# Reordering within a step of a graph attention and mixture-of-experts kernel: place transposes, factor products and counts later on TensorE, factor sums and tile results earlier on VectorE

## The chip, the core and the metric

The kernel runs on one core of a Trainium2 chip. A core has five engines with a queue of instructions each: TensorE (PE in the profile, its weight loads PEld), VectorE (DVE), ScalarE (ACT), GpSimd (POOL) and SyncE (SP), which here only starts transfers. The metric is the device time of one execution in microseconds (us), the median of several runs.

## The reference

6250 nodes with 256 features and 100000 edges go through a graph attention layer with two heads of 128 features, and then through a feed-forward layer in which every node is given to one of eight experts. Cut to what matters:

```python
x = x + gnn(layernorm(x))           # 6250 x 256
x = x + ffn(layernorm(x))

# gnn: Wh = x @ W_w + W_b, two heads of 128
e     = leaky_relu(s[src] + t[dst])     # s, t: one number per node and head
alpha = softmax of e over the edges of one src
agg   = segment_sum(alpha * Wh[dst], src)
out   = where(deg > 0, agg, Wh)

# ffn
H      = gelu(x @ W1 + b1)              # 6250 x 1024
probs  = softmax(H @ Wg + bg)           # 8 experts
assign = argmax(probs)
out    = probs[assign] * (H @ Wd[assign] + bd[assign])
```

## The kernel before

All main work is in `common_path`. A second function, `general_path`, is entered only for inputs that the first can't do, and isn't run here.

First, a start stage of some 115 us sorts the edges by source and writes a table of the projected nodes (260 numbers a row) to DRAM. Then the nodes are taken in 49 blocks of 128 source nodes. For every block the kernel needs up to 15 ranks of edges: rank t holds one edge for each of 128 lanes. GpSimd gathers the destination rows of each rank from the table with an indirect transfer (`fetch`, L788, L792), in three portions of five ranks. Of the 15 ranks 12 are taken straight from a sorted window; the last three, the "late ranks", collect what didn't fit and are picked out by products on TensorE.

The pieces of a block that the change concerns are these:

- `gather_late` (L733): six matmul instructions (three products) that move late edges to their lanes (tile pm, L738).
- `choose` (L740, L745 to L756): VectorE picks the late edges out; ScalarE casts their places into `loc` (L756).
- `spread` (L758): TensorE transposes the places of all 15 ranks (L761), ScalarE casts them to lT (L763), SyncE writes them to DRAM (lrow, L765) and reads them back for all partitions (lbc, L767).
- `compare` (L769, L771): VectorE turns lbc into a mask of ones and zeros, in place. There is a single buffer for lbc.
- `factors` (L773, L779): 15 small products of the mask with the source nodes' terms. `factor_sums` (L782, L786): VectorE adds the three pieces of each product.
- `count_pairs` (L685, L691): eight products that count edges to frequent destinations, from masks that `pick_pairs` (L677, L681 and L682) made.
- `compare_back` and `weigh` (L806, L814) on VectorE and ScalarE weight the gathered rows with the factor sums; `add_up` (L828, L833) sums them on TensorE into the block's result; `finish` (L836) normalizes it.

Four blocks make a phase k of the feed-forward layer: norm (`g_norm`), turns (`g_turn`, L903, that is, transposes of the normalized tokens), the hidden layer (`g_hidden`, L916), the experts' logits (`g_logits`, L954, `g_fold`, L966), the choice of expert (`g_choose`, `g_count`, `g_place`), and then turned rows (`g_rows`, L1039 and L1040) that `g_send` scatters into a list for each expert in DRAM. Tiles of 128 rows of those lists are read back (`w_load`, L1126), turned (`w_turn`, L1039), multiplied with the expert's weights (`w_expert`, L1144 and L1146), and finished on VectorE by `w_out` (L1158 and L1160, result y), whose result `w_wait` stores. PSUM tiles named pf, three in number, serve all of this part: each turn, product or count takes one and gives it back when another engine has read it. PSUM tiles named pm, two in number, serve the late ranks, places, factors and counts.

The order of the work is written out by hand. `at(slot, place, fn, ...)` files every piece under a step (slot) and a place within the step; the list is sorted by both, and each engine runs its instructions in that order. Block b stands at u = 3b, so that a block takes three steps and a phase twelve; v is the step in which phase k begins. The pieces of many blocks share a step: for instance, in every third step `spread` of one block stands beside `add_up` of an earlier one and, in one step of twelve (v+1), beside the token turns of a phase (place 38) and the turned rows of the phase before (places 38 and 39). On ScalarE, the copies of the turned rows and the rest of a row (L1040, L1055) have the places of their rows, the turned tokens (L908) have 45, and the cast in `choose` has 16. In steps v+7 and v+10 `g_fold` and `g_count` (36) and more turned rows (38) meet `spread`. Tiles of a phase are turned in steps 5, 7, 9 and 11 of the next phase's twelve, and their `w_out` follows two steps later.

Of the kernel before, what the change touches and what calls it, by code (L numbers as in the profile page):

```python
# [36 lines left out]
def common_path(  # L37
# [57 lines left out]
    NPH = -(-(NB - 1) // FB) + 1  # L95
# [98 lines left out]
    with ExitStack() as edges:  # L194
# [3 lines left out]
        def at(slot, place, fn, *args):  # L198
            plan.append((slot, place, len(plan), fn, args))
# [311 lines left out]
        for i, (d, flip) in enumerate(steps):  # L511
            t = 11 + 1.7 * i if i < 18 else 41.6 + 1.02 * (i - 18)
# [16 lines left out]
        for f0, f1, t0, step in ((n0, n1, 8.0, 0.7), (n4, NB - 1, 15, 2.0)):  # L529
            for j, b in enumerate(range(f0, f1)):  # L530
                c = b % CH
                t = t0 + step * (j - 0.5 * c)
# [11 lines left out]
        for b in range(NB):  # L544
            t = XN0 + NODE * b
# [374 lines left out]
        def blocks_of(k):  # L920
            return range(max(0, (k - 1) * FB + 1), min(NB, k * FB + 1))
# [268 lines left out]
        for b in range(NB):  # L1190
            u = 3 * b
            at(u - 6, 46, window, b)
            at(u - 4, 24, measure, b)
            at(u - 4, 43, prefix, b)
            at(u - 3, 5, prefix_out, b)
            at(u - 3, 12, split, b)
            at(u - 3, 33.7, gather_late, b)
            at(u - 2, 17, pick_pairs, b)
            at(max(u - 1, -0.2), 63, load_terms, b)
            at(u, 56, scale_terms, b, 0)  # L1200
            at(u + 1, 56, scale_terms, b, 1)
            at(u, 34, count_pairs, b)
            at(u + 2, 51, weigh_pairs, b)
            at(u + 4, 31, add_pairs, b)
            at(u - 2, 16, choose, b)
            at(u - 2, 33.5, spread, b)
            at(u, 9, compare, b)
            at(u, 33, factors, b)
            at(u + 1, 47, factor_sums, b)
            at(u + 4, 62, owned, b)  # L1210
            at(u + 6, 13, owned_biased, b)
            for q in range(3):
                at(u + q, 30, fetch, b, q)
                at(u + q + 1, 48, compare_back, b, q)
                at(u + q + 1, 50, weigh, b, q)
                at(u + q + 3, 32, add_up, b, q)
            at(u + 6, 14, finish, b)

        worked = n_off = 0
        u = [3 * blocks_of(k)[-1] + 6 for k in range(NPH)]  # L1220
        for k in range(NPH):
            bs = blocks_of(k)
            v = u[k]
            last = k == NPH - 1
            at(v, 34 if last else 51, g_norm, k)
            for i in range(-(-len(bs) // 2)):
                at(v + 0.5 * i, 52, g_xn, k, i)
                at(v + 1, 38 + 0.1 * i, g_turn, k, i)
                at(v + 1, 45 + 0.1 * i, g_turned, k, i)
            for q in range(4):  # L1230
                at(v + 2 + q, 20, g_hidden, k, q)
            at(v + 6, 19, g_logits, k)
            at(v + 6, 56, g_logits_out, k)
            at(v + 7, 36, g_fold, k)
            at(v + 8, 12, g_bias, k)
            at(v + 8, 35 if last else 51, g_max, k)
            at(v + 8, 58, g_exp, k)
            at(v + 9, 35 if last else 51, g_choose, k)
            at(v + 10, 36, g_count, k)
            at(v + 11, 35 if last else 51, g_place, k)  # L1240
            for i in range(len(bs)):
                t, p = (((v + 6, 40), (v + 6, 41), (v + 8, 60), (v + 8, 61))[i] if last else
                        ((v + 10, 38), (v + 11, 38), (v + 13, 38), (v + 13, 39))[i])
                at(t, p, g_rows, k, i)
                at(max(t, v + 10), p, g_rest, k, i)
                at(v + 14 if i > 1 and not last else v + 12, 44, g_send, k, i)
            rows_in = min(N, (bs[-1] + 1) * P)
            n = (TILES if last else max(0, (rows_in - LAG) // P)) - worked
            worked += n
            if n == 0:  # L1250
                continue
            assert n <= NMAX
            n_off += n if k < NPH - 2 else 0
            todo = tabulate(k, n, last)
            for i in range(2):
                at(*((v + 12, 35) if last else (v + 12 + 3 * i, 53)), next, todo)
            for i in range(n):
                t = v + 15 + i if last else u[k + 1] + (5 + 8 * i // n if k < NPH - 2 else (10, 11, 12, 13, 14)[i])
                at(t - 1 if last else t - 2 if k == NPH - 2 else max(t - 3, v + 15), 46 if last else 64, w_load, k, i)
                at(t, 21, w_turn, k, i)  # L1260
                at(t + 1, 22, w_expert, k, i)
                at(t + 2, 30 if k < NPH - 2 else 36, w_out, k, i)
                at(t + 2, 45, w_send if k >= NPH - 2 else w_wait, k, i)
        at(v + 18, 47, judge)
        for j in range(-(-n_off // 2)):
            t = 3 * NB + 4 + j + (7 if j > 9 else 0)
# [7 lines left out]
@with_exitstack  # L1274
def gat_then_ffn_kernel(
    ctx: ExitStack,
    tc: tile.TileContext,
    x: bass.AP,
    src: bass.AP,
    dst: bass.AP,  # L1280
    W: bass.AP,
    Wb: bass.AP,
    a: bass.AP,
    W1: bass.AP,
    b1: bass.AP,
    Wg: bass.AP,
    bg: bass.AP,
    Wd: bass.AP,
    bd: bass.AP,
    out: bass.AP,  # L1290
):
    keep = ctx.enter_context(tc.tile_pool(name="keep", bufs=1))
    odd = keep.tile([1, 1], I32, name="odd")
    common_path(tc, x, src, dst, W, Wb, a, W1, b1, Wg, bg, Wd, bd, out, odd)
    flag = tc.nc.values_load(odd[0:1, 0:1], min_val=0, max_val=1,  # L1295
                             skip_runtime_bounds_check_because="a flag, 0 or 1")
    with tc.If(flag > 0):
        general_path(tc, x, src, dst, W, Wb, a, W1, b1, Wg, bg, Wd, bd, out)
# [506 lines left out]
```

## Time and profile before

| | us |
|---|---|
| median of 3 runs | 1344.82 |
| lowest and highest | 1343.49, 1346.52 |
| the profiled execution | 1348.73 |
| its span (first to last instruction) | 1346.9 |
| mean granted TensorE clock | 0.924 |

| stage of the span, us | PE busy | DVE busy | ACT busy | POOL busy |
|---|---|---|---|---|
| 60 to 120 | 43.40 | 46.72 | 42.10 | 6.71 |
| 300 to 400 | 81.21 | 76.20 | 52.20 | 76.40 |
| 700 to 800 | 90.88 | 75.30 | 57.31 | 75.67 |
| 1100 to 1200 | 91.88 | 74.33 | 56.52 | 68.58 |
| 1250 to 1300 | 47.05 | 11.91 | 11.89 | 23.95 |

A line of waits reads "engine, tile, line <- what ended the wait: us in total, times, longest". A line of the timeline reads "start, duration, engine, line, operation, output<-input, number of instructions", and in brackets the idle time before it and what ended that. L761 means line 761 of the kernel. "issue" is time in which the engine waited for nothing that the profile shows. The start stage ends at about 115 us, the gathers end at 1194.1 us, and the rest is the last phase's feed-forward work.

### The profile page before, as it was taken

The numbers are of one execution on the slowest core, as the hardware profiler recorded it, in microseconds if no ns is written. First come the engines' busy times: TensorE is split into PE (matmuls) and PEld (weight loads), VectorE is DVE, ScalarE is ACT, GpSimd is POOL, SyncE is SP. The second block draws the span as 40 slices with busy tenths as digits, with TensorE's granted clock in tenths as the row PEclk, the third lists the DMA queues.
The fourth block names the chain that finished last, engine by engine and source line by source line (L and its number), as shares of the span: only waits on it lengthen the run. The fifth ranks groups of instructions, "written<-read, shape, count | busy, mean of one in ns | idle before, by whom it ended". The sixth has DMA issues, their size and how long they took to land. (4 is left out here: it accounts for less than half of the span.)

```text
span 1346.9 us, 22461 instructions
## 1 busy us (share of the span) xinstructions
PE 1130.7 (84%) x6404; PEld 864.5 (64%) x6404; DVE 945.8 (70%) x3521; ACT 694.2 (52%) x2060; POOL 877.9 (65%) x990
## 2 busy tenths in 40 slices
PE   4683667777986998989979989899898998998997
PEld 3462555556674775775856757757676677585785
DVE  6986877868687787786777876968777779652311
ACT  4683344544645455546465565564645555645321
POOL 0005777777777777776777777777776767736362
PEclk9796887897997998998999999999998899899998
DMA  4764776765656566665766656666657566646871
GB/s 143 220 198 133 228 208 168 207 195 152 187 156 204 182 204 181 221 180 178 219 208 186 216 172 199 198 203 202 213 178 208 158 193 190 182 155 236 296 251 54
DMA packets 118428, 257.91 MB, mean 191 GB/s; under 512 B 24254, under 2 KB 70538, under 8 KB 118152
## 3 DMA queue, kind: packets, MB, share of 16 engines
q0 software_dynamic: 46544, 137.57, 34.2%
q1 hardware_dynamic: 64440, 111.76, 26.3%
q10 hardware_dynamic: 7312, 7.05, 1.6%
q8 instruction: 55, 0.90, 0.3%
q14 instruction: 77, 0.63, 0.2%
HBM read 205.03 MB, written 57.98 MB: 195 GB/s over the span
## 5 line engine op out<-in xcount | busy, mean ns | idle before, releaser
L792 POOL DMA_INDIRECT wg<-table,dsti x735 | 717.0, 976 | 238.4 <-issue 190.4
L833 PE MATMUL p_a<-wg,hot 128*128 128x258 f32 x1470 | 365.5, 399 | 0.0
L833 PEld LDWEIGHTS p_a<-wg,hot 128*128 128x128 f32 x1470 | 286.5, 201 | 52.0 <-issue 9.2
L826 ACT ACTIVATE wg<-wg 128x128 f32<-128x128 f32 x735 | 230.9, 390 | 4.8
L916 PE MATMUL pf<-xT,w_sb 128*128 128x512 f32 (+1 forms) x416 | 200.1, 630 | 22.7 <-ACT xT L908 22.7
L1146 PE MATMUL pf<-wd_sb,half 128*128 x880 | 206.3, 388 | 0.0
L1146 PEld LDWEIGHTS pf<-wd_sb,half 128*128 128x128 f32 x880 | 163.9, 191 | 37.0 <-issue 11.6
L824 ACT COPY wg<-fix 128x10 f32<-128x10 f32 x147 | 25.0, 170 | 297.0 <-DVE wg L823 232.2
L916 PEld LDWEIGHTS pf<-xT,w_sb 128*128 128x128 f32 x416 | 81.3, 210 | 109.5 <-issue 80.6
L809 DVE TENSOR_TENSOR hot<-fix,loc 128x640 f32<-128x640 f32 x147 | 119.1, 810 | 32.7 <-ACT wg L824 32.7
L823 DVE TENSOR_TENSOR wg<-wg,fix 128x640 f32<-128x640 f32 x147 | 120.7, 821 | 5.1
L918 ACT ACTIVATE hT<-pf,b_sb 128x512 f32<-128x512 f32 (+1 forms) x104 | 67.9, 659 | 55.1 <-PE pf L916 54.9
L1040 ACT COPY half<-pf 128x512 f32<-128x512 f32 x110 | 61.4, 585 | 65.9 <-PE pf L1146 34.3
L1040 ACT COPY row<-pf 128x512 f32<-128x512 f32 x94 | 52.4, 586 | 55.0 <-PE pf L1039 54.5
L1060 POOL DMA_INDIRECT by_expert<-row,place_i x47 | 46.8, 996 | 51.1 <-ACT half L1040 17.5
L771 DVE TENSOR_SCALAR lbc<-lbc,iota_p 128x1920 bf16<-128x1920 bf16 x49 | 36.1, 737 | 61.2 <-DMA lbc<-lrow 61.2
L456 PE MATMUL pf<-w_sb,xT 128*128 128x260 f32 x196 | 61.1, 441 | 19.0 <-ACT xT L450 19.0
L704 ACT ACTIVATE wt<-tm,hot_e 128x128 f32<-128x128 f32 x196 | 66.5, 386 | 8.1 <-DMA tm<-terms 8.1
L1039 PE MATMUL pf<-ident,hT 128*128 128x128 f32 x392 | 59.3, 289 | 13.3 <-ACT row L1040 13.2
L619 POOL DMA_INDIRECT win<-keys,first x49 | 48.5, 989 | 32.1 <-DMA keys<-keyb 14.2
L1039 PEld LDWEIGHTS pf<-ident,hT 128*128 128x128 f32 x392 | 46.8, 148 | 21.3 <-ACT row L1040 18.5
L1039 PE MATMUL pf<-ident,row 128*128 128x128 f32 x312 | 45.2, 283 | 18.1 <-DVE y L1160 12.4
(274 smaller groups left out, 1746.9 us busy)
## 6 DMA issues: line engine op xcount, KB each, us to landing
row<-by_expert SPq DMA_DIRECT2D x39, 641.0 KB
lbc<-lrow SPq DMA_DIRECT2D x49, 480.0 KB
wg<-table,dsti POOLq DMA_INDIRECT x735
wg<-by_expert SPq DMA_DIRECT2D x16, 641.0 KB
wd_sb<-in_L_ffn_Wd_dram SPq DMA_DIRECT2D x8, 1024.0 KB
tm<-terms SPq DMA_DIRECT2D x49, 128.0 KB
table<-tb ACTq DMA_DIRECT2D x12, 520.0 KB
xs<-in_x_dram SPq DMA_DIRECT2D x12, 512.0 KB
```

The source lines that it names most:

```text
L456: nc.tensor.matmul(pW[:, :TW], xT[:, k * P:(k + 1) * P], w_sb[:, k, :], start=(k == 0), stop=(k == KC - 1))
L704: nc.scalar.activation(kept[b]["wt"][:, g, h, :], tm[:, h, :], AF.Identity, scale=hot_e[:, g, 1, h:h + 1])
L792: nc.gpsimd.indirect_dma_start(out=wg[:, t - QS[q], :], out_offset=None, in_=table[:, :], in_offset=bass.IndirectOffsetOnAxis(ap=kept[b][" ...
L809: nc.vector.tensor_tensor(hot[:, :n], iota_ps.unsqueeze(1).to_broadcast([P, n, P]), kept[b]["loc"][:, QS[q]:QS[q + 1]].unsqueeze(2).to_bro ...
L823: nc.vector.tensor_mul(wg[:, :, :D], wg[:, :, :D], p_w[:, :, 0:1].to_broadcast([P, n, D]))
L826: nc.scalar.activation(wg[:, t, D2:SE], wg[:, t, D2:SE], AF.Identity, scale=wg[:, t, D + 1:D2])
L833: nc.tensor.matmul(sums[b], hot[:, t - QS[q], :], wg[:, t - QS[q], :SE], start=(t == 0), stop=(t == T - 1))
L916: nc.tensor.matmul(ph[:, :w], wt["w1"][:, k, j * P:(j + 1) * P], xT[:, k, :w], start=(k == 0), stop=(k == KC - 1))
L918: nc.scalar.activation(hT[:, j, :w], ph[:, :w], AF.Gelu, bias=wt["b1"][:, j:j + 1])
L1039: nc.tensor.transpose(pT[:, j * P:(j + 1) * P], rows(4 * h + j), ident)
L1040: nc.scalar.copy(o, pT)
L1146: nc.tensor.matmul(py[:, :C], res[k]["half", i, j // 4][:, j % 4, :], wt["wd"][:, ds(wo[0] + j * C, C)], start=False, stop=(j == KH - 1))
```

## The change

Six calls of `at` get other places; the functions themselves stay as they are, and every piece stays in its step.

```diff
-            at(u - 3, 33.7, gather_late, b)
+            at(u - 3, 40, gather_late, b)
...
-            at(u, 34, count_pairs, b)
+            at(u, 43, count_pairs, b)
...
-            at(u - 2, 33.5, spread, b)
+            at(u - 2, 40, spread, b)
             at(u, 9, compare, b)
-            at(u, 33, factors, b)
-            at(u + 1, 47, factor_sums, b)
+            at(u, 42, factors, b)
+            at(u + 1, 10, factor_sums, b)
...
-                at(t + 2, 30 if k < NPH - 2 else 36, w_out, k, i)
+                at(t + 2, 11 if k < NPH - 2 else 36, w_out, k, i)
```

On TensorE the late ranks, place transposes, factor products and counts now come after the places 36 to 39 of their step, where folds, expert counts, token turns and turned rows stand. In a step that has late ranks, factors and counts together, the order was factors, late ranks, counts, and is late ranks, factors, counts. `spread` takes ScalarE's cast and SyncE's two transfers with it. On VectorE factor_sums stood between `pick_pairs` and `compare_back` of its step and now stands ahead of `choose`; `w_out` of all but the last two phases stood after the late-rank work of its step and now stands ahead of it.

## The prediction, written before the changed kernel was run

> **What bounds the kernel now.** I read the page's busy table first, then the totals of who waited for whom, then one repeating stretch in order of time.
>
> ```profile
> PE 1130.7 (84%) x6404; PEld 864.5 (64%) x6404; DVE 945.8 (70%) x3521; ACT 694.2 (52%) x2060; POOL 877.9 (65%) x990
> ```
>
> ```profile
> POOL wg L792 <- issue: 190.4, 609, 1.9
> DVE lbc L771 <- DMA lbc<-lrow: 61.2, 23, 4.5
> DVE pick L662 <- ACT late L653: 53.0, 20, 5.0
> PE pm L761 <- ACT loc L756: 40.5, 18, 5.7
> PE pf L916 <- ACT xT L908: 22.7, 13, 2.0
> DVE col L745 <- PE pm L738: 15.6, 11, 2.7
> PE pf L1039 <- DVE y L1160: 12.4, 8, 2.3
> ```
>
> No engine is full by the busy table, but two are nearly so. GpSimd's 190.4 us of "issue" is 0.3 us after each gather: a gather costs 0.976 + 0.30 us, and 68 indirect transfers (60 gathers, 4 windows, 4 row sends) are the 86.8 us that GpSimd needs for four blocks. TensorE takes longer. The place transposes (L761) of blocks 27, 31, 35 and 39 start at 693.7, 782.6, 871.8 and 960.5: 88.9, 89.2 and 88.7 us for the same four blocks. The gathers end at 1194.1, but the sums that use the last of them start at 1211.0. So TensorE trails, and from about 400 us on (before it GpSimd paces) a round of twelve steps, 89 us long, sets the time; 794 us are 8.9 rounds. In GpSimd's timeline the waits above that 0.30 sum to 24 us between 529 and 1187: that is all that a faster round can win before GpSimd is the limit.
>
> The round is a chain over several engines. Let v be the step in which a phase of four blocks starts its norm. Here is step v+1 of block 27 (start, duration, what it waited for), first TensorE, then ScalarE:
>
> ```profile
> 693.70 0.28 PE L761 MATMUL pm<-ident,loc 128*15 128x128 f32 x1 [1.75 <-ACT loc L756]
> 693.81 1.04 PE L1039 MATMUL pf<-ident,hT 128*128 128x128 f32 x8
> 695.30 1.09 PE L903 MATMUL pf<-ident,xnf 128*128 128x128 f32 x8 [0.45 <-DVE y L1160]
> 696.23 0.60 PE L1039 MATMUL pf<-ident,hT 128*128 128x128 f32 x4
> 697.51 0.66 PE L1039 MATMUL pf<-ident,hT 128*128 128x128 f32 x4 [0.67 <-ACT row L1040]
> 700.12 1.13 PE L916 MATMUL pf<-xT,w_sb 128*128 128x512 f32 x2 [1.95 <-ACT xT L908]
> ```
>
> ```profile
> 693.46 0.18 ACT L756 CAST loc<-late_i 128x3 f32<-128x3 int32 x1
> 694.01 0.26 ACT L763 CAST lT<-pm 15x128 bf16<-15x128 f32 x1 [0.37 <-PE pm L761]
> 694.45 1.07 ACT L1040 COPY row<-pf 128x512 f32<-128x512 f32 x2 [0.18 <-PE pf L1039]
> 698.99 1.07 ACT L908 COPY xT<-pf 128x512 f32<-128x512 f32 x2
> ```
>
> TensorE waits 1.75 us for VectorE's choice of late ranks (through ScalarE's cast, L756), and the row and token turns stand behind that wait. The hidden layer (L916) then waits for ScalarE. In step v+11 a turn waits for a tile result:
>
> ```profile
> 764.30 0.48 DVE L1160 SCALAR_TENSOR_TENSOR y<-pf,row 128x256 f32<-128x256 f32 x1
> 764.83 1.09 PE L1039 MATMUL pf<-ident,row 128*128 128x128 f32 x8 [1.59 <-DVE y L1160]
> ```
>
> **What the Trainium skill says.** "PSUM — Partial Sum Buffer", section "Engine vs sequencer instructions": ScalarE's and VectorE's queues are strictly first in, first out, and matmuls run in program order. The trace agrees: the row copies of 694.45 stood behind lT, which waited 0.37 us. "DMA: Bandwidth & Descriptors", section "Two DMAs through the same engine are not ordered": a DMA that reads what another wrote needs the first one's semaphore. Agreed: lbc is issued only after lrow has landed (lrow 761.70, lbc 763.54), so a late transpose delays both transfers. "Perfetto Trace Analysis", section "Optimization Strategy": a gap that repeats can mean too few buffers for the next tile. Agreed: the waits for y and the 0.67 us for a row copy recur every round, and the turns share three pf tiles.
>
> **The change, part by part** (per round, v+1 to v+12).
>
> Spread, 33.5 to 40: one transpose (0.28), ScalarE's cast lT (0.26), two SP transfers. It moves only in three of four blocks. Nothing on SP or GpSimd is passed; behind its two transfers on SP wait the y stores, own, tm and tile loads.
> - Step v+1, behind 24 turns. TensorE can start the row turns at 692.0, when its sums end, instead of 693.8. But ScalarE's queue still has the cast L756 ahead of the row copies, and now factor_sums (0.24) and w_out (0.15 + 0.47, overlapped) run before choose, as DVE reaches it at 692.1: 0.65 us later, the cast ends at 694.3. Row copies then start at 694.35 (0.10 sooner, as lT has left their front), end 695.4; the second token turn follows the first copy, the last rows the second; copies end 698.15, rest 698.5, lT 698.75, xT 699.85. L916 starts at 699.9: **-0.2**, not -1.75.
> - Step v+4: nothing lies between; 0.
> - Step v+7: behind the fold (0.96). That mask lands 0.95 later; VectorE already waits 1.91 for it at 750.1 (L771). It shifts VectorE's run up to its wait at 771.7 (1.13, for L653), which takes it in: 0. That cover gone, it costs 0.95.
> - Step v+10: behind count (0.05) and eight row turns with one wait (0.68), and lT behind the row copies: about 2.7 later. lbc was issued 763.5, goes to 766.2, and lands 4.1 to 4.4 later (as where VectorE waits for it): 770.5, where VectorE asks at 769.8. The 0.7 lie inside the same 1.13; where that wait was 0.3 to 0.5 (blocks 26, 34, 46) some 0.5 stay: **+0.1** on average.
>
> Factors 33 to 42, counts 34 to 43, late ranks 33.7 to 40: in their steps the three only swap (late ranks first; 0.52, 0.83 and 0.61 us). They add no wait for the split's pick, which was ready 4 us earlier (pick's end 731.6, products 735.9). Factor_sums at 10 now heads VectorE's step and waits for the products; behind it stand choose, dests, compare_back and weigh, and for them the casts and sums. Only in step v+7 is VectorE early (1.15 wait for L738): choose comes 0.7 later there, and the place transpose started 3.7 us after its cast: 0, at worst 0.7 (cover gone), not below 0, as nothing is taken out.
>
> w_out, 30 or so to 11 (0.6 us, 4 per round): y comes 1.0 sooner in v+11 (L633 to L642 were ahead), nearly 3 in v+1 and v+7. In v+11 the wait of 1.59 could fall to 0.6, but VectorE is up to 0.95 late there by the mask of v+7: between -1.0 and +0.1. In v+7 a turn waits 0.91 for a logits copy (L960); with y's pf tile free at 737.9 it could use that one: -0.9 or 0, as the tile is dealt. The two don't add fully, since the later wait takes up the earlier gain. I take **-0.3**.
>
> Sum: -0.2 + 0.1 - 0.3 = -0.4 us a round, x 8.9 = **-3.6 us**. The start (GpSimd-paced to 400) and the tail (no moved step after 1190; w_out of the last two phases stays; the last factor_sums, which waited 2.5 us, now holds up one w_out whose tile nobody wants for 4 us) give 0. The profiled execution lasted 1348.73 us, 1.8 around its span of 1346.9, and is 3.9 above the median; 1348.73 - 3.6 = 1345.1 there, and from the median 1344.82 - 3.6 = **1341.2**.
>
> **Rivals.**
> 1. *The gates stay* (ScalarE's cast and the mask): gains and delays cancel, -0.3 to +0.3 a round, 1342.1 to 1347.5. For it: the cast keeps its place 16. Chance 0.24.
> 2. *TensorE wins its waits whole*: 1.75 + 0.45 + 1.59 = 3.8 a round, cut by GpSimd's floor at about -2, some -12 to -24 in all: 1321 to 1333, say 1328. Against it: ScalarE's order above. Chance 0.10.
> 3. *Slower: the late mask*. Where lbc of steps v+7 and v+10 lands later than the 0.3 to 1.13 us that VectorE waits afterwards can absorb, every later VectorE instruction up to the choice in v+1, which is itself 0.65 later, is late, then ScalarE and L916. It decides once the transposes slip by over 2.5 us. Price 0.7 a round, x 8.9 = +6.2: 1351. For it: 61.2 us of waits for lbc already. Chance 0.29.
> The forecast's own range, 1334 to 1342 (0.3 to 1.2 us a round), has 0.37.
>
> **Numbers.** Faster by over 0.2% (2.7 us, about what a measurement here tells from none): 0.37 + 0.10; same 0.24; slower 0.29. For 8 in 10 I leave out most of rival 2 below 1331 and the end of rival 3 above 1353.
>
> **What would show it.** After: L761's wait for L756 gone in v+1, yet L916 starting only about 0.2 sooner after the cast; L771 waiting more, L662 less; y ahead of choose. It is wrong if rounds differ by over 1 us from 89, if L771's waits rise without L662's falling (rival 3), or if L916's wait on L908 shrinks (rival 2).

## The result, and the profile after

On the chip of the prediction the changed kernel takes **1336.02 us** (median of 19 runs, 1328.92 to 1342.49) beside 1346.39 us for the kernel before (19 runs, 1337.12 to 1354.38): a ratio of 0.9925, 95% interval 0.9904 to 0.9947, or -10.4 us. The forecast was faster by 3.6 us (ratio 0.9973), in a range of 1331 to 1353. The sign and the range held. The size didn't: 0.9973 lies outside the interval. Every ratio here is of the faster executions of the two kernels, those within 1.5% of each kernel's fastest (on this chip all of them), while the profiles of e3, e4 and e9 below caught slower ones.

The profiled execution after lasted 1333.79 us, with a span of 1332.0. First the busy table and the totals of waits of the changed kernel (engine, tile, line, what ended the wait, us in total, times, longest):

```profile
PE 1119.5 (84%) x6404; PEld 854.5 (64%) x6404; DVE 949.3 (71%) x3521; ACT 690.3 (52%) x2060; POOL 878.3 (66%) x990
```

```profile
DVE lbc L771 <- DMA lbc<-lrow: 80.2, 42, 4.6
...
PE pf L916 <- ACT wg L824: 20.6, 11, 2.0
...
PE pf L1039 <- DVE y L1160: 15.3, 16, 2.1
...
DVE pick L662 <- ACT late L653: 14.1, 13, 2.2
...
PE pf L903 <- ACT row L1040: 12.2, 11, 1.9
...
PE pm L761 <- ACT loc L756: 7.6, 7, 2.2
...
PE pf L916 <- ACT xT L908: 2.6, 2, 2.0
```

Read against the lines of before, this is a list of waits that changed their names. L761's 40.5 us are 7.6. L771 waits 19.0 us longer for the mask, and L662 38.9 less. L916 waited 22.7 for L908 and now waits 20.6 + 2.6, put down mostly to L824, the next record on ScalarE. L903 waits for row copies, and y still costs 15.3 us, in 16 places instead of 8. Of L761's 40.5 us, 26.8 lie ahead of 430 us, where L738, which now has place 40, waits 23 us more after the change (33.3 instead of 9.9).

So where are the 14.9 us between the two spans? I let the steady part begin with the kernel's fourth hidden layer (L916). It starts at 429.1 before and 425.8 after (3.3 us sooner), the eight rounds from there are 12.8 us shorter, and the rest is 1.2 longer. Here are those stretches in the two kernels, before and then after (window, its length, TensorE's busy time, instructions, granted clock, the DMA engines' share, GB/s):

```profile
429.10:1151.50 722.40, 653.13 (x3856) 0.96 0.64 195
1151.50:1346.90 195.40, 177.09 (x920) 0.97 0.58 196
```

```profile
425.80:1135.40 709.60, 643.34 (x3857) 0.97 0.64 198
1135.40:1332.00 196.60, 178.71 (x920) 0.97 0.60 199
```

TensorE does the same work in both and is busy 9.8 us less, at a granted clock of 0.97 instead of 0.96. Its idle time fell from 69.3 to 66.3 us, by 3.0, which is **0.38 us a round**. A round is 90.3 us before and 88.7 after (means; single rounds are 87.8 to 93.7 before and 85.4 to 90.8 after); 1.2 of these 1.6 us are busy time.

The busy time follows the clock closely. In both profiles the granted clock is full or half and nothing between, and in the rounds it changes by windows of 3.41 us. Half rate takes 60.7 us of the eight rounds before and 40.6 after. Half of the difference, 10.1 us, is the work that TensorE could not do in that time; the measured difference in busy time is 9.8. Half rate comes where TensorE has just stood idle. Here are two neighbouring windows of the kernel before, behind the wait of 1.77 us for y in v+11 of an early round (columns as above):

```profile
581.99:585.40 3.41, 1.55 (x12) 1.00 0.67 190
585.40:588.81 3.41, 3.41 (x10) 0.50 0.82 229
```

In the first, TensorE is idle for 1.86 us of 3.41; in the second it has no idle time and runs at half rate. Within the eight rounds of both kernels the clock drops from full to half 20 times, and 19 times TensorE had been idle for 1.76 us or more of the window ahead (once 1.35). It stays full 369 times, and in only four of these was the window ahead as idle (1.80 to 1.89 us). Before the change five of the drops come within 1.6 us of the end of a wait of 1.77 to 2.30 us for the cast L756 or for y (at 513.7, 585.4, 605.9, 1032.6 and 1145.2); after it none does, although TensorE waits up to 2.10 us for y in v+9 there. Most of the others, in both kernels, lie behind the turns of v+1 and the wait of L916.

I split the idle time of a round by its steps (gaps between TensorE's records, mean of the eight rounds):

| idle of TensorE, us a round | before | after |
|---|---|---|
| v+7 | 0.65 | 0.77 |
| v+9 | 0.09 | 1.34 |
| end of v+10 and v+11 (row turns) | 2.22 | 0.77 |
| behind v+11, before L1144 | 1.03 | 1.31 |
| v+1, to the start of L916 | 4.67 | 4.09 |
| sum | 8.66 | 8.28 |

In v+1 (TensorE, then ScalarE, after):

```profile
680.21 0.63 PE L903 MATMUL pf<-ident,xnf 128*128 128x128 f32 x4 [0.27 <-DVE col L745]
682.00 0.66 PE L903 MATMUL pf<-ident,xnf 128*128 128x128 f32 x4 [1.16 <-ACT row L1040]
...
684.31 0.27 PE L761 MATMUL pm<-ident,loc 128*15 128x128 f32 x1
686.56 1.98 PE L916 MATMUL pf<-xT,w_sb 128*128 128x512 f32 x4 [1.98 <-ACT wg L824]
```

```profile
681.26 0.19 ACT L756 CAST loc<-late_i 128x3 f32<-128x3 int32 x1 [0.32 <-DVE late_i L755]
681.36 1.07 ACT L1040 COPY row<-pf 128x512 f32<-128x512 f32 x2
```

The place transpose (L761) waits for nothing any more. The turns wait instead: for the row copies, which stand behind the cast L756 on ScalarE.

In v+9 the order of turn and y has changed. Before, both halves of the turn run without a wait, 5 us ahead of that step's y:

```profile
749.48 1.19 PE L1039 MATMUL pf<-ident,row 128*128 128x128 f32 x8
```

```profile
754.64 0.47 DVE L1160 SCALAR_TENSOR_TENSOR y<-pf,row 128x256 f32<-128x256 f32 x1
```

After the change, here are TensorE's turns of v+9 and of the end of v+10, and VectorE in v+9 and v+11:

```profile
739.03 0.66 PE L1039 MATMUL pf<-ident,row 128*128 128x128 f32 x4 [1.25 <-DVE y L1160]
...
751.57 0.66 PE L1039 MATMUL pf<-ident,hT 128*128 128x128 f32 x4 [0.72 <-DVE y L1160]
...
752.18 1.39 PE L1039 MATMUL pf<-ident,row 128*128 128x128 f32 x8
```

```profile
737.59 0.94 DVE L771 TENSOR_SCALAR lbc<-lbc,iota_p 128x1920 bf16<-128x1920 bf16 x1 [1.81 <-DMA lbc<-lrow]
...
738.51 0.47 DVE L1160 SCALAR_TENSOR_TENSOR y<-pf,row 128x256 f32<-128x256 f32 x1
...
751.04 0.47 DVE L1160 SCALAR_TENSOR_TENSOR y<-pf,row 128x256 f32<-128x256 f32 x1
```

In v+11 the turn (752.18) finds y done since 751.51 and waits for nothing, where it waited 1.59 before. The turn that waits for y is now the last half of v+10's row turn, at 751.57. There a row copy ended at 751.48, too, so this round alone can't tell which of the two it waited for. But in five of the eight rounds the half starts 0.05 to 0.06 us after y's end and ahead of the copy's, as here (TensorE, then ScalarE; y ends at 576.21, the copy at 576.40):

```profile
576.26 0.66 PE L1039 MATMUL pf<-ident,hT 128*128 128x128 f32 x4 [0.49 <-DVE y L1160]
```

```profile
575.81 0.59 ACT L1040 COPY row<-pf 128x512 f32<-128x512 f32 x1 [3.11 <-PE pf L1039]
```

So this half took the tile that y frees, where before the change it waited 0.68 for the row copy. The wait of 1.25 in v+9 is new as well. The row turn's second half takes the tile that y frees, and y stands behind the mask (L771), which waits for lbc. Before the change the turn of v+9 ran ahead of that y, so it took other tiles. My reading is that w_out had place 30, behind the turn's 21 in the order in which tiles are dealt, and now has 11. That isn't shown: in v+11 of the kernel before, a turn with place 21 did start 0.05 us after the end of a y with place 30, in all eight rounds.

Both waits go back to the mask. VectorE has no gap over 0.15 us between the mask's start in v+9 and y's end in v+11, neither before (750.12 to 764.78) nor after (737.59 to 751.51), and after the change y of v+11 ends 12.3 to 12.5 us behind y of v+9 in all eight rounds.

### The profile page after: what moved, and what is told of

It reads as the page before. It is cut to its first block, busy times and chain, and to the rows that moved or that the text cites. A ratio compares the mean times of both kernels' runs of the same rounds, so it can differ in the third digit from the quotient of the medians.

```text
span 1332.0 us, 22441 instructions
## 1 busy us (share of the span) xinstructions
PE 1119.5 (84%) x6404; PEld 854.5 (64%) x6404; DVE 949.3 (71%) x3521; ACT 690.3 (52%) x2060; POOL 878.3 (66%) x990
## 5 line engine op out<-in xcount | busy, mean ns | idle before, releaser
L833 PE MATMUL p_a<-wg,hot 128*128 128x258 f32 x1470 | 361.4, 395 | 0.0
L916 PE MATMUL pf<-xT,w_sb 128*128 128x512 f32 (+1 forms) x416 | 196.4, 620 | 23.2 <-ACT wg L824 20.6
L824 ACT COPY wg<-fix 128x10 f32<-128x10 f32 x147 | 24.5, 167 | 278.8 <-DVE wg L823 216.4
L916 PEld LDWEIGHTS pf<-xT,w_sb 128*128 128x128 f32 x416 | 80.0, 208 | 109.3 <-issue 79.2
L809 DVE TENSOR_TENSOR hot<-fix,loc 128x640 f32<-128x640 f32 x147 | 118.9, 809 | 22.8 <-ACT wg L824 22.5
L1040 ACT COPY half<-pf 128x512 f32<-128x512 f32 x110 | 61.2, 585 | 78.5 <-PE pf L1039 42.4
L771 DVE TENSOR_SCALAR lbc<-lbc,iota_p 128x1920 bf16<-128x1920 bf16 x49 | 36.2, 738 | 80.2 <-DMA lbc<-lrow 80.2
L1040 ACT COPY row<-pf 128x512 f32<-128x512 f32 x94 | 52.2, 585 | 54.1 <-PE pf L1039 53.1
L1039 PE MATMUL pf<-ident,hT 128*128 128x128 f32 x392 | 58.4, 285 | 15.1 <-ACT row L1040 7.8
L738 PE MATMUL pm<-rest,pick 128*128 128x29 f32 x294 | 40.8, 275 | 33.3 <-DVE place_i L666 18.8
L738 PEld LDWEIGHTS pm<-rest,pick 128*128 128x128 f32 x294 | 42.8, 206 | 39.8 <-issue 33.0
```

Of the source, the lines that this page charges most:

```text
L738: nc.tensor.matmul(pk[:, c, :], k["pick"][:, c * P:(c + 1) * P], k["rest"], start=True, stop=True)
L809: nc.vector.tensor_tensor(hot[:, :n], iota_ps.unsqueeze(1).to_broadcast([P, n, P]), kept[b]["loc"][:, QS[q]:QS[q + 1]].unsqueeze(2).to_bro ...
L833: nc.tensor.matmul(sums[b], hot[:, t - QS[q], :], wg[:, t - QS[q], :SE], start=(t == 0), stop=(t == T - 1))
L916: nc.tensor.matmul(ph[:, :w], wt["w1"][:, k, j * P:(j + 1) * P], xT[:, k, :w], start=(k == 0), stop=(k == KC - 1))
L1039: nc.tensor.transpose(pT[:, j * P:(j + 1) * P], rows(4 * h + j), ident)
L1040: nc.scalar.copy(o, pT)
```

## The experiments

e1 to e8 ran on one chip and e9 to e12 on another, and that has to be known to read them. Which chip the result comes from isn't on record; by the times I take it for a third. Both chips of the experiments are alike, and slower: the kernel before takes 1681.83 and 1680.12 us in two sessions on the one and 1678.26 on the other, at a mean clock of 0.846. In the profiles of the experiments a round takes 114 to 120 us instead of 90, and VectorE stops for up to 18 us where the profile names nothing of the program that it waits for. There is no profile of the kernel before on these chips. So only ratios to the kernel before, each with its 95% interval, are compared. They are some 0.3% wide on either side.

Two theories at first. **A**: the gain is spread's, since its wait held TensorE's turns up to 5.7 us in early rounds. **B**: the gain is w_out's, since y frees a pf tile. A third, **C**, gives it to late ranks and products.

**e1 and e8**, spread alone:

```diff
-            at(u - 2, 33.5, spread, b)
+            at(u - 2, 40, spread, b)
```

> The kernel before with spread alone moved (33.5 to 40). Theory A (the wait of the place transpose for VectorE's choice held TensorE's turns, and longest in rounds before 690 us, up to 5.7 us, where I counted only 1.75): ratio 0.993 to 0.996, that is -5 to -9 us, L761 gone from TensorE's waits. Theory B (w_out carries the gain): within 0.1% of before. As forecast (-0.1 a round): -0.9 us, ratio 0.9993.

> spread alone moved, a second time, beside the others on one chip. If it repeats: 0.992 to 0.997. My forecast for this part: 0.9993.

Measured 0.9943 (0.9917 to 0.9969) and 0.9959 (0.9931 to 0.9987). Alone, spread gains 0.4 to 0.6% there. That is what A expects, and more than the 0.07% forecast.

**e2 and e7**, w_out alone:

```diff
-                at(t + 2, 30 if k < NPH - 2 else 36, w_out, k, i)
+                at(t + 2, 11 if k < NPH - 2 else 36, w_out, k, i)
```

> The kernel before with w_out alone moved (30 to 11). Theory A: -1 to -3 us, ratio 0.998 to 0.999, and PE pf L1039 <- DVE y shorter. Theory B (an earlier y frees the pf tile in three places of every round): -5 to -9 us, ratio 0.993 to 0.996. As forecast (-0.3 a round): -2.7 us, ratio 0.998.

> w_out alone moved, a second time, beside the others on one chip. If it repeats: 0.989 to 0.994. My forecast for this part: 0.998.

Measured 0.9914 (0.9886 to 0.9941) and 0.9916 (0.9891 to 0.9942). That is what B expects and more (0.993 to 0.996), four times the forecast's 0.2%. A and B can't both be whole, so the next one asks whether they add.

**e5**, spread and w_out (the two edits above):

> The kernel before with spread and w_out moved, the rest left. If the parts add (0.9943 and 0.9914 alone, and 1.0058 for late ranks, factors, counts and sums), this is faster than the whole change: ratio 0.984 to 0.988. If the two moves win the same wait (a TensorE that comes to its turns earlier meets the other gate), it is no better than the better of the two alone: 0.990 to 0.994.

Measured 0.9916 (0.9880 to 0.9952). They don't add: beside w_out, spread is worth nothing that can be seen here.

**e3**, late ranks, factors, counts and sums:

```diff
-            at(u - 3, 33.7, gather_late, b)
+            at(u - 3, 40, gather_late, b)
...
-            at(u, 34, count_pairs, b)
+            at(u, 43, count_pairs, b)
...
-            at(u, 33, factors, b)
-            at(u + 1, 47, factor_sums, b)
+            at(u, 42, factors, b)
+            at(u + 1, 10, factor_sums, b)
```

> The kernel before with late ranks, factors, counts and factor sums moved as in the change, spread and w_out left. Theories A and B: no gain, ratio 0.999 to 1.003, as the sums now wait for the products at the head of VectorE's step. Theory C (late ranks out of the way of folds and counts is what gains): ratio 0.994 to 0.997. As forecast: 0.

Measured 1.0058 (1.0036 to 1.0080): slower, so C falls. The loss is also more than A and B expected (1.003 at most).

**e4**, the change without spread's part:

```diff
-            at(u - 2, 40, spread, b)
+            at(u - 2, 33.5, spread, b)
```

> The changed kernel with spread put back to 33.5 (all else as changed). Theory A: most of the gain is gone, ratio 0.997 to 1.000. Theory B: most of it is kept, 0.992 to 0.995. As forecast: it loses 0.9 us of what the change gives.

Measured 0.9959 (0.9931 to 0.9988), between A's numbers and B's. The whole change (e9, below) has 0.9948: the change without spread gains 0.1% less, which the intervals don't tell from nothing. That speaks against A.

**e6**, the change with factor_sums put back:

```diff
-            at(u + 1, 10, factor_sums, b)
+            at(u + 1, 47, factor_sums, b)
```

> The changed kernel with factor_sums back at 47. If what the third part loses is factor_sums waiting for the late products at the head of VectorE's step, with choose and weighing behind it, this one is 0.3% or more below the changed kernel: ratio to before 0.985 to 0.989. If the loss is TensorE's (products later for their own sake), it stays at 0.991 to 0.995.

Measured 0.9932 (0.9907 to 0.9956), by its number the second case. The third part seems to cost less without the sums' move, but the difference from e9 is within the intervals, so which of the two moves loses isn't decided.

**e9**, the whole change:

> The whole change, beside the parts on one chip. If the parts win the same waits (w_out alone 0.9915, spread and w_out 0.9916) and the rest only costs a little: 0.991 to 0.996. If the parts added, it would be 0.988 or below. My forecast for the whole: 0.9973.

Measured 0.9948 (0.9919 to 0.9977), at a mean clock of 0.846, the same as the kernel before. That is the first case: the parts overlap. w_out alone (0.9914 and 0.9916) lies below the whole, but the intervals overlap.

The profiles, one for each run, hint at where e3 loses. In the runs with factor_sums at 10 (e3, e4, e9) the last sum of gathered rows ends 26.7 to 27.4 us after the last gather. In all but one of the others it is 18.0 to 18.8. The exception is e12, below, with 26.4. Here is VectorE at its last factor sums, first in e12, then in e6:

```profile
1511.75 0.25 DVE L786 TENSOR_REDUCE fs<-pm 128x30 f32<-128x90 f32 x1 [9.19 <-remote]
```

```profile
1491.39 0.25 DVE L786 TENSOR_REDUCE fs<-pm 128x30 f32<-128x90 f32 x1 [3.30 <-PE pf L1039]
```

"remote" is a release that the profile can't put down to anything of this core that it recorded; in e3, e4 and e9 this stop is 10.8 to 11.5 us. If every execution has it, these 9 us at one place are nearly all of e3's loss (1692.11 - 1681.83 = 10.3). On the first chip the same stretch is 19.4 us before and after, and VectorE there waits 2.5 and 4.5 us for L691. So the loss may belong to the later chips' stops, and what the move would cost without them may be close to the forecast's 0. No run took the stop away, and e9, which has it, lies only 0.16% above e6, which doesn't.

Next, where in the round w_out gains. **e10** moves it only in v+7 and v+1:

```diff
-                at(t + 2, 30 if k < NPH - 2 else 36, w_out, k, i)
+                at(t + 2, 36 if k >= NPH - 2 else 11 if t % 3 == 2 else 30, w_out, k, i)
```

> w_out at 11 only in steps v+7 and v+1, where it stood behind the choice of late ranks and the pair masks; at 30 in v+9 and v+11. If the choice's wait for TensorE's late products is what kept the pf tile: nearly all of w_out's gain, 0.991 to 0.994. If the gain is in v+11, the 1.59 us wait that I costed highest: 0.996 to 1.000.

Measured 1.0012 (0.9979 to 1.0045): nothing, although y starts 9 to 10 us earlier there than in e11, below, which leaves it at 30 in these steps (2.6 instead of 11.5 us after the expert's products in v+7, about 5 instead of 15 in v+1; means over rounds). It seems that nothing on the path wanted those tiles.

**e11** moves it only in v+9 and v+11:

```diff
-                at(t + 2, 30 if k < NPH - 2 else 36, w_out, k, i)
+                at(t + 2, 36 if k >= NPH - 2 else 30 if t % 3 == 2 else 11, w_out, k, i)
```

> The other half: w_out at 11 in v+9 and v+11, at 30 in v+7 and v+1. The choice's wait as the cause: 0.997 to 1.000. v+11 as the cause: 0.991 to 0.995.

Measured 0.9905 (0.9877 to 0.9933): the whole of w_out's gain. Of the two steps, v+11 has y no sooner (a mean of 5.5 us after the products in e10, 6.3 in e11, over seven rounds that lie between 0 and 12); v+9 has it at 2.6 us instead of 7.9. Step v+9 of one round, TensorE and VectorE, in e10 and then in e11:

```profile
1057.95 0.66 PE L1039 MATMUL pf<-ident,row 128*128 128x128 f32 x4 [1.57 <-ACT late L653]
```

```profile
1058.57 0.42 DVE L662 TENSOR_SCALAR pick<-iota_s,late 128x384 f32<-128x384 f32 x1
...
1062.36 0.48 DVE L1160 SCALAR_TENSOR_TENSOR y<-pf,row 128x256 f32<-128x256 f32 x1
```

```profile
1044.73 0.66 PE L1039 MATMUL pf<-ident,row 128*128 128x128 f32 x4 [0.92 <-issue]
```

```profile
1044.20 0.48 DVE L1160 SCALAR_TENSOR_TENSOR y<-pf,row 128x256 f32<-128x256 f32 x1
1044.67 0.55 DVE L662 TENSOR_SCALAR pick<-iota_s,late 128x384 f32<-128x384 f32 x1
```

In e10, y stands behind the split's pick (L662) and ends some 5 us after the tile of the late counts (L653) is free. The second half of the row turn takes that tile, and waits for it. In e11, y is ahead of the pick, and the turn's second half starts at 1044.73, when y has ended at 1044.68. It has still waited 0.92 us, so 0.65 of the 1.57 are won. So, as on the first chip, moving w_out has changed which tile the turn takes (read from these starts, not seen directly); but here the tile that it used to take comes late itself. In the totals of e10 this wait stands as

```profile
PE pf L1039 <- ACT late L653: 9.1, 7, 2.0
```

and it is gone in e11. There 5.5 us more of L1039's waits are put down to "issue" (22.5 us in 15 places instead of 17.0 in 10), so part of the wait has only changed its name, and what is left is far from the 16 us that e11 gains. L650's and L903's waits for row copies (L1040) are 6.3 and 7.6 us smaller in e11. That the earlier y in v+9 is the cause of these wasn't tried by itself: e11 moved v+9 and v+11 together.

**e12** moves w_out alone, and further:

```diff
-                at(t + 2, 30 if k < NPH - 2 else 36, w_out, k, i)
+                at(*((t + 1, 49) if k < NPH - 2 else (t + 2, 36)), w_out, k, i)
```

> w_out alone moved still further, to place 49 of the step before, ahead of the weights' last three operations (fe, fix, wg). If every microsecond by which the pf tile comes free sooner counts: below w_out at 11, 0.985 to 0.990. If getting out from behind the choice was all that counted: 0.990 to 0.994, the same as at 11. If the result now delays the weighing: above 0.994.

Measured 0.9992 (0.9964 to 1.0021), by its number the third case. But 8.4 us of the profiled run are the stop at the end that e12 shares with e3; without it, by an estimate that takes it to be in every execution, it would be near 0.994. So it doesn't decide what an earlier y is worth.

## Why the prediction was right in sign and too small

- **v+1.** "L916 starts at 699.9: -0.2, not -1.75" was the right mechanism: the place transpose lost its wait, ScalarE's cast kept its place, and the turns now wait behind it. The size was -0.58 (4.67 to 4.09). My step placed L916 5.6 us after the cast's end; it measured 6.48 before and 5.11 after. Rival 2's 1.75 did not come, and L916's wait on L908 (22.7 us) shrank only in name.
- **The mask.** L771 waits 19.0 us more and L662 38.9 less: on VectorE the later mask was taken in by a wait that was there anyway, as the prediction said for v+7 and v+10. Rival 3 needed the opposite. But the prediction followed the mask to VectorE's next wait only, and not to y, which stands between the two (next point).
- **w_out in v+9 and v+11.** For v+11 the prediction gave "between -1.0 and +0.1" and for v+9 nothing. Measured, the wait of v+11 is gone whole (-1.45 for the two steps' row turns), and v+9 has a new one (+1.25). The two belong together: VectorE goes without a gap from the mask of v+9 to y of v+11, so TensorE waits once for that run, now in v+9 and little in v+11. With v+9's wait taken out, TensorE would by this reading come to the row turn at the end of v+10 1.25 us sooner and wait that much longer for y there. The net is -0.2, beside the -0.3 that I took. The prediction asked "as the tile is dealt" for v+7 only; it was v+9 where the deal changed, and through it the late mask, rival 3's mechanism, reached TensorE.
- **w_out in v+7.** "-0.9 or 0": +0.12, and e10 finds nothing. The 0 was right.
- **Factors, late ranks, counts, sums at 0.** On the first chip nothing in the steps or the tail (19.4 us and 19.4 us) speaks against it. On the later chips they cost 0.58% alone, perhaps most of it one stop.
- **The sum.** -0.58 - 1.45 + 1.25 + 0.12 + 0.28 = -0.38 us a round, where the forecast said -0.4. Some of the agreement is luck: spread gave more than forecast and two waits that I had not seen took it back.

**What the sum missed** is the rest. It priced each wait at its own length and took TensorE's busy time as given. Of the 14.9 us between the two profiled spans, 9.8 are busy time of the same instructions in the eight rounds, and 3.0 are idle time. The failed step is therefore the last one, "-0.4 us a round, x 8.9": the waits came out at 0.38 a round in the profile, but the medians moved by nearly three times 3.6 us, and the clock, which the sum put at nothing, is the larger part of what the profiles show. In them half rate follows windows of 3.41 us in which TensorE was idle for about half of the time, so a long wait can cost more than its length: a window at half rate loses 1.7 us of work. That the two waits the change removed (L756's and y's, up to 2.3 us) brought 5 of the 12 drops before is read from their places; no run removed the idle time alone.

How much of the 10.4 us of the medians is clock is **open**. It is a matter of some 20 us at half rate in two single executions, and the windows don't fall alike in every round: in the rounds of 693.7 to 960.5, from which the forecast took its 89 us, a wait of 1.75 to 1.89 for L756 brought no half rate. The kernel before has a clock on record for one run alone there (0.924); the 19 runs after have 0.925 to 0.939, mean 0.931. On the later chip both kernels have 0.846, and the change still gains 0.5% there. So it has a gain that needs no higher clock, but its waits there are others (v+9), and it can't be carried over. The prediction's own sign of being wrong, rounds over 1 us from 89, can't be used: five of the eight rounds after are, but so are five of those before; the forecast had read three even ones (88.7 to 89.2).

The experiments point to w_out alone in v+9 and v+11 (0.9905) as at least as good as the whole (0.9948), both on the same chip; the intervals overlap. On the first chip it wasn't run. There, by the working above, keeping w_out at 30 in v+9 would probably only move the wait to the end of v+10, and an earlier mask would be the thing to try.

## What to carry to other kernels

Taking one wait off a chain of several engines mostly renames it: L761's wait went from 1.7 us a round (13.7 in eight rounds) to none, and the rounds' idle time fell by 0.38 us of 8.66. Split the idle time by step before and after, and compare the busy time and the granted clock too: here two thirds of the difference between two profiles lay there, and the drops of the clock stood behind TensorE's longest waits. Where a few buffers are dealt in turn, an instruction that frees one and is moved ahead of an allocation changes who waits for which: write out the deal anew for every step it passes, also for those that had no wait.

## What the runs showed of the hardware that was not expected

- TensorE's granted clock drops to half for 3.41 us or a few times that, and 19 of 20 drops in the rounds of both profiles follow a window of 3.41 us with 1.76 us or more of idle time. No single idle time there was longer than 2.31 us. The slower chips show the same: in e1, between 500 and 1450 us, 35 of 40 drops follow a window with 1.7 us or more of idle time, and one of the 159 windows that stay full does.
- The same kernel takes 1345 us in the first runs and 1680 on the two chips of the experiments, and the clock (0.924 against 0.846) is the smaller part: TensorE is busy 1251.8 us in e1 and 1130.7 before, 121 more, while the span is 330 longer (1677.0 and 1346.9). In between, engines stop where the profile names no cause in the program. VectorE stopped for "remote" 19 times before L745 in e1, 137.7 us in all, up to 17.2, and never in the first chip's two profiles.
- These stops move with the order of the instructions: with factor_sums heading the step it is L786 that has them (138.3 us, 17 times, in e9). What they are, no run here shows.
